# Four joint edits to a macaron kernel of four layers: the first mixture's routing in program order and its table between the experts, a pipelined weight product, another combine and lag, and an expert input built slice by slice

## The chip, the core and the metric

The kernel runs on one core of a Trainium2 chip. The metric is the device time of one launch in microseconds (us). The core has a matrix engine (TensorE, PE in the profile), a vector engine (VectorE, DVE), a scalar engine (ScalarE, ACT), a general engine (GpSimd, POOL) and a queue engine that only issues transfers (SyncE, SP). Each engine executes its own list of instructions in order; semaphores let one wait for another. Everything is fp32.

## The reference

x is 4 sequences of 512 tokens with 128 features. Four layers follow; each is a half-weighted feed-forward part, an attention (or a scan), and the same feed-forward part again with the same weights:

```python
x = x + 0.5 * _L0_ffn_ref(_layernorm(x), ...)   # Switch mixture: 8 experts, one choice, capacity 320
x = x + _L0_attn_ref(_layernorm(x), ...)        # 16 heads, a table of relative positions
x = x + 0.5 * _L0_ffn_ref(_layernorm(x), ...)
x = x + 0.5 * _L1_ffn_ref(_layernorm(x), ...)   # SwiGLU mixture: all 8 experts, two chosen, and a shared one
x = x + _L1_attn_ref(_layernorm(x), ...)        # factorised scores
x = x + 0.5 * _L1_ffn_ref(_layernorm(x), ...)
x = x + 0.5 * _L2_ffn_ref(_layernorm(x), ...)   # 8 linear experts, top two
x = x + _L2_attn_ref(_layernorm(x), ...)        # decay scan
x = x + 0.5 * _L2_ffn_ref(_layernorm(x), ...)
x = x + 0.5 * _L3_ffn_ref(_layernorm(x), ...)   # mixture, two choices a token, capacity 512
x = x + _L3_attn_ref(_layernorm(x), ...)
x = x + 0.5 * _L3_ffn_ref(_layernorm(x), ...)
```

A mixture of layer 0 or 3 does, for each token: logits of 8 experts, a softmax, the best expert (or two), the token's place within that expert by a running count over all tokens, and, if the place is under the capacity, relu(token w1 + b1) w2 + b2, weighted with the softmax value. In layer 2 an expert is linear, so its two weights can be multiplied into one 128x128 matrix beforehand. The table of layer 0's attention adds `table[t - s]` per head to the scores.

## The kernel before

**Mixtures.** The four mixture passes of layers 0 and 3 are objects named f00, f01 (layer 0) and f30, f31 (layer 3). Their names end the names of tiles, shown in the profile without numbers as `_f`. A pass has these stages.

- `empty` and `clear` (L288, L293) write zeros into two DRAM areas: disp, where tokens are put in the order of experts, and res, where answers are put in the order of tokens.
- `tokens` (L296) handles one or more sequences and yields between steps: GpSimd writes token numbers beside the tokens (L307); `norms` (L160) makes statistics on VectorE (L168, L169), the inverse root on GpSimd (L172, L173, and L176, L177 where ScalarE will apply it), and the normalised rows on VectorE, ScalarE, both, or GpSimd, as the argument `on` says; TensorE transposes (L195) and multiplies with the gate (lg, L330); VectorE picks the expert (mx, eq, first, masks; L344, L228 to L234); a scan and three small products count the places (pre L362, rank L373 to L379); VectorE makes the row to write to (kept, at, slot, to; L400 to L409); GpSimd sends the rows with one indirect transfer per 128 tokens and choice (L416), 16 for layer 0 and 32 for layer 3. Sequences depend on each other only through `cum`, the running count.
- `experts` (L426) fetches an expert's rows from disp on SP's queue (`fetch`, L443, two experts ahead), transposes them (`prepare`, L452: dT), multiplies with w1 (h, L487, 8 products of 128x320 for an expert of layer 0), bias and relu on ScalarE and VectorE, prepares the next expert, calls `beside` if there is one, multiplies with w2 (o, L523), adds the bias, weights, and sends the answers out by an indirect transfer (L509). With two choices, an expert's rows are in two halves, d and d2, filled from opposite ends; `prepare` multiplies the second with 0 or 1 (`behind`) and adds it to the first.
- `combine` (L533) reads the answers of a sequence back (r) and adds them to x.

**Order.** Most of the kernel is given to a scheduler that orders each engine's instructions by readiness within pools; `tc.manual_schedule(engines=...)` keeps the order of the program on the engines that it names. `skewed(gens, lag)` (L1519) goes round several step-by-step parts: part i joins in round i x lag. `whole` runs a part to its end. PSUM's 8 banks and the staging pool `stage` (5 buffers named raw) are handed round in order.

**The launch** (L1554 to L1570). The relative positions are fetched, disp is zeroed, then four parts `choices`, one for each sequence, are made, with norms on ScalarE and VectorE in turn. The first runs four steps; then comes the second part of `prep_table` (L945), which zeroes the table on VectorE (L953), sums the embeddings and writes the rows to DRAM (tab_rows); then all expert weights (`moe_weights`, L542, fetches in pairs of experts); then the zeros of res; then the rest of the choices, two steps apart. Behind that comes the last part of `prep_table`: eight times, two heads are fetched as overlapping rows (rev), turned over by one product (turned, L976) and copied into the table. `prep_l0_attn` transposes the attention's weights, and `padded_values` fills vpad with GpSimd (L582). Only then come f00's experts.

**After f01** (L1579 to L1603). `prep_l2` fetches layer 2's weights while f01's experts run, as their `beside`. When they are done it takes, for each expert, four transposes (wo2T, L1326), a copy that goes to ScalarE or VectorE in turn (`copy`, L131), four accumulating products (m, L1331), and a copy. A sigmoid of one column is put on ScalarE (L1585), which loads the table of that function ahead of its use. Then `combine` adds f01's answers to all four sequences, and `l1_ffn` runs for the two pairs of sequences, the second pair 12 rounds behind the first: norms (n), transposes (T), logits (lg, L1066), the up products (gu, L1151, L1152), the choice of two experts (`chosen`, L1075: comb), the transpose of that (gT, L1127), which goes through DRAM to be spread (rows, cb), and the down products (o, L1186). The first pair is `followed` by the beginning of layer 1's attention.

**f30's choices** (L1612 to L1623). Sequences 0 and 1 route inside the chain of layer 2. Sequences 2 and 3 route at its end, the second three steps behind the first, with GpSimd's order that of the program.

Of the kernel before, what the change touches and what calls it, by code (L numbers as in the profile page):

```python
# [17 lines left out]
P = 128  # L18
# [5 lines left out]
E = 8  # L24
# [17 lines left out]
def kernel(ctx: ExitStack, tc: tile.TileContext, a: dict, out: bass.AP):  # L42
# [202 lines left out]
    class Mixture:  # L245
# [180 lines left out]
        def experts(self, w, beside=None):  # L426
# [3 lines left out]
            with tc.tile_pool(name=f"moe_{self.tag}", bufs=2) as pool:  # L430
# [21 lines left out]
                def prepare(e):  # L452
                    tag = f"{e}_{self.tag}"
                    d = got[e, 0]
                    if self.k == 2:
                        d2 = got[e, 1]
                        nc.vector.tensor_tensor(d2, d2, bc(behind[:, e, :], [P, per, W]), ALU.mult)
                        nc.vector.tensor_tensor(d[:, :, :D], d[:, :, :D], d2[:, :, 2:], ALU.add)
                        nc.vector.tensor_tensor(d[:, :, D:], d[:, :, D:], d2[:, :, :2], ALU.add)
                    ps = bank(f"dT{tag}")  # L460
                    for s in range(per):
                        m = min(P, cap - s * P)
                        nc.tensor.transpose(ps[:, s * P : s * P + m], d[:m, s, :D], ident[:m, :m])
                    dT = pool.tile([P, cap], FP, name=f"dT{tag}", tag="dT")
                    nc.scalar.copy(dT, ps[:, :cap])  # L465
# [479 lines left out]
    def prep_table(pool):  # L945


        rel = stage.tile([P, D], FP, name="rel", tag="rel", bufs=1)
        nc.sync.dma_start(rel, a["L0_attn_rel_pos_emb"][P - 1 : 2 * P - 1, :])
        yield  # L950

        table = pool.tile([P, NH, S], FP, name="table", tag="table", bufs=1)
        nc.vector.memset(table[:, :, : S - 2 * P], 0.0)  # L953
# [12 lines left out]
        yield  # L966

        for h in range(0, NH, 2):

            rev = stage.tile([P, 2, 2 * P], FP, name=f"rev{h}", tag="raw")  # L970
            nc.sync.dma_start(
                rev,
                bass.AP(tensor=rows.tensor, offset=rows.offset + h * 3 * P, ap=[[1, P], [3 * P, 2], [1, 2 * P]]),
            )
            ps = bank(f"turned{h}")
            nc.tensor.matmul(ps, flip, rev.rearrange("p h s -> p (h s)"), start=True, stop=True)  # L976
            copy(table[:, h : h + 2, S - 2 * P :], ps.rearrange("p (h s) -> p h s", h=2))
        l0["table"] = table
        yield

    def prep_l0_attn():
        qkv = head_weights(a["L0_attn_qkv_w"], a["L0_attn_qkv_b"], "l0")
# [313 lines left out]
    def prep_l2(pool):  # L1296

        l2["gate"] = load_T(a["L2_ffn_w_gate"], E, D, "gate2T")
        l2["w_in"] = load(a["L2_attn_W_in"], [P, 2 * D], "win2")
        l2["w_out"] = load(a["L2_attn_W_out"], [P, D], "wout2")  # L1300
        l2["b_out"] = load_row(a["L2_attn_b_out"], "bout2")
        l2["b_in"] = load_T(a["L2_attn_b_in"].rearrange("(k d) -> k d", k=2), 2, D, "bin2T")
        yield

        m = pools["w"].tile([P, E, D], FP, name="m2", tag="m2")
        l2["m"] = m
        got = {}

        def fetch(e):
            wi, wo = raw[:, 0, e].rearrange("p (c d) -> p c d", d=D), raw[:, 1, e]  # L1310
            nc.sync.dma_start(wi, a["L2_ffn_w_in"][e].rearrange("(c f) d -> f c d", f=P))
            nc.sync.dma_start(wo, a["L2_ffn_w_out"][e])
            got[e] = wi, wo

        raw = pool.tile([P, 2, E, FF], FP, name="raw2", tag="raw2")
        for e in range(E):

            behind = yield
            nc.gpsimd.tensor_copy(raw[0:1, :, e, 0], behind[0:1, 0:1].to_broadcast([1, 2]))
            fetch(e)  # L1320
        yield
        for e in range(E):
            wi, wo = got[e]
            ps = bank(f"wo2T_{e}")
            for c in range(NC):
                nc.tensor.transpose(ps[:, c * P : (c + 1) * P], wo[:, c * P : (c + 1) * P], ident)  # L1326
            woT = pool.tile([P, FF], FP, name=f"wo2T_{e}", tag="woT", bufs=3)
            copy(woT, ps)
            pm = bank(f"m2_{e}")
            for c in range(NC):  # L1330
                nc.tensor.matmul(  # L1331
                    pm[:, :D], wi[:, c, :], woT[:, c * P : (c + 1) * P], start=(c == 0), stop=(c == NC - 1)
                )
            copy(m[:, e, :], pm[:, :D])

    def l2_ffn(pool, i, bs):
        tag = f"f2{i}_{bs[0]}"
# [215 lines left out]
    with tc.tile_pool(name="tables", bufs=1) as tables:  # L1553
        f00 = Mixture("f00", CAP0, 1)  # L1554
        f00.zeroed(stage, "raw", 5)
        made = prep_table(tables)
        next(made)
        whole(f00.empty())
        with tc.tile_pool(name="routing00", bufs=2) as pool:
# [12 lines left out]

        f30 = Mixture("f30", CAP3, 2)
        l0_attn(f00.combine, emptied(f01, f30), lambda b: f01.tokens([b], gate0T, fine=True))
    with tc.tile_pool(name="weights12", bufs=1) as mid:
# [7 lines left out]
            whole(made)  # L1583
        first = small.tile([P, 1], FP, name="first_sigmoid", tag="first_sigmoid", bufs=1)
        nc.scalar.activation(first, l2["m"][:, 0, 0:1], AF.Sigmoid)  # L1585
        for b in range(NB):
            whole(f01.combine(b))
        with tc.tile_pool(name="ahead1", bufs=2) as ahead:
            vpads[:] = [padded(ahead, 0), None]
            begun = l1_begin(ahead)  # L1590

            def followed(pool, bs):
                yield from l1_ffn(pool, 0, bs)
                if bs[0] == 0:

                    yield from begun[0](0)
                    for g in range(2):
                        begun[1](0, g)
                        yield
                        begun[4][0, g] = begun[2](0, g)  # L1600

            with tc.tile_pool(name="ffn10", bufs=2) as pool:
                whole(skewed([followed(pool, bs) for bs in pairs], 12))  # L1603

            early = []
            with tc.tile_pool(name="gates10", bufs=1) as pool:
                l1_attn(
                    lambda _: prep_l3_ffn(xs[0]), begun,
                    lambda b: l1_early(pool, pairs[0], early) if b == 1 else iter(()),
                )  # L1610

        def behind(pool, bs):  # L1612
            yield from l1_ffn(pool, 1, bs, early if bs[0] == 0 else None)
            yield from l2_ffn(pool, 0, bs)
            yield from l2_attn(pool, bs)
            yield from l2_ffn(pool, 1, bs)
            if bs[0] == 0:

# [77 lines left out]
```

## Time and profile before

| | us |
|---|---|
| time before, median of 3 (1512.09 to 1516.94) | 1515.85 |
| the profiled execution | 1516.03 |
| its span, and what lies outside it | 1514.3, 1.7 |
| PE busy, of the span | 1278.2 (84%) |
| VectorE, ScalarE, GpSimd busy | 881.6, 682.6, 696.5 |
| mean granted TensorE clock | 0.914 |
| routing of f00; its experts | 0 to 62; 62 to 112 |
| layer 0's attention | 115 to 346 |
| f01's scatters and experts; prep_l2's products | 346 to 423; 419 to 443 |
| first feed-forward part of layer 1; its attention | 423 to 520; 520 to 820 |
| chain of layers 1 to 2; f30's scatters and experts | 820 to 972; 972 to 1084 |
| layer 3's attention; f31 | 1084 to 1395; 1395 to 1515 |

The page lists the busy time of each engine, the span in 40 slices, the chain of work that ended last (each step followed back to what released it), and the costliest groups. In a row of the timeline, the columns are start, duration, engine, line, operation, result, operands with their shapes, and count; in brackets stands how long the engine sat idle before it and what ended that. These rows of the page belong to the stages above:

```profile
L509 POOL DMA_INDIRECT res_f<-y_f,back_f x112 | 109.7, 980 | 127.6 <-ACT y_f L508 91.3
L416 POOL DMA_INDIRECT disp_f<-n_f,to_f x96 | 95.1, 991 | 55.8 <-issue 37.1
L487 PE MATMUL h_f<-dT_f,w_l 128*128 128x320 f32 (+1 forms) x256 | 104.0, 544 | 2.8 <-ACT dT_f L465 2.8
```

They read: 96 scatters kept GpSimd busy for 95.1 us, 991 ns each; and TensorE waited only 2.8 us in all ahead of the 256 first products of the experts, all of it for the copy of dT.

### The profile page before, as it was taken

How to read it: one execution, taken by the hardware profiler on the slowest of the kernel's cores; microseconds unless marked ns; L12 is line 12 of the kernel's file. 1: busy time of each engine (PE TensorE's matmuls, PEld its weight loads, DVE VectorE, ACT ScalarE, POOL GpSimd, SP SyncE). 2: the span in 40 equal slices, each digit the busy share in tenths (PEclk: the TensorE clock that was granted, in tenths of full speed). 3: DMA queues.
4: the chain of work that ended last, by engine and by line, in shares of the span. 5: the costliest groups of instructions: out<-in, count | busy, mean ns of one | idle time of the engine just before them, and what ended most of it. 6: DMA issues, size and time to landing. Idle time of an engine off the chain costs nothing.

```text
span 1514.3 us, 28772 instructions
## 1 busy us (share of the span) xinstructions
PE 1278.2 (84%) x10645; PEld 817.5 (54%) x10645; DVE 881.6 (58%) x2893; ACT 682.6 (45%) x1431; POOL 696.5 (46%) x808
## 2 busy tenths in 40 slices
PE   4687999995968989998999878739589999998394
PEld 3464666774755656676656656627333434343273
DVE  5336777663356657777566755434287787772343
ACT  1235877871422367776621222104336555563041
POOL 5346767871533578876443112555520323202253
PEclk9898999996989999999999887759799999998597
DMA  8410240002412874241130000032114000000223
GB/s 259 104 53 22 79 171 11 9 7 78 147 36 57 230 241 151 85 142 36 38 76 1 1 0 3 29 90 85 49 42 149 9 12 5 15 1 15 78 82 108
DMA packets 100660, 106.21 MB, mean 70 GB/s; under 512 B 9084, under 2 KB 73832, under 8 KB 100520
## 3 DMA queue, kind: packets, MB, share of 16 engines
q1 hardware_dynamic: 91752, 90.11, 20.7%
q0 software_dynamic: 6656, 13.22, 2.5%
q8 instruction: 84, 1.38, 0.4%
q10 hardware_dynamic: 2112, 1.05, 0.3%
q14 instruction: 56, 0.46, 0.1%
HBM read 62.49 MB, written 41.85 MB: 69 GB/s over the span
## 4 chain that ended last, share of the span: by engine, by line
PE 66%; DVE 9%; POOL 8%; issue 7%; DMA 6%; ACT 2%; SPq 1%; POOLq 0%; ACTq 0%; DVEq 0%
PE s_a L618 13%; PE t_a L663 8%; PE h_f L487 5%; PE acc_a L757 5%; PE o_f L523 5%; PE acc_a L685 5%; PE y_f L1380 4%; PE t_a L618 3%; PE ot_a L776 2%; POOL disp_f L416 2%; POOL res_f L509 2%; PE gate_f L1397 2%; PE lg_f L330 1%; PE T_f L195 1%; DVE low L707 1%
## 5 line engine op out<-in xcount | busy, mean ns | idle before, releaser
L650 POOL TENSOR_SCALAR sc_a<-sc_a,top_a 128x128 f32<-128x128 f32 (+3 forms) x256 | 276.5, 1096 | 84.4 <-DVE top_a L635 58.5
L618 PE MATMUL s_a<-k_a,q_a 32*128 32x512 f32 (+3 forms) x1536 | 262.7, 540 | 5.4 <-DVE top_a L639 3.5
L727 ACT ACTIVATE w_a<-t_a 128x512 f32<-128x512 f32 x256 | 140.2, 595 | 124.2 <-PE t_a L618 92.1
L707 DVE TENSOR_REDUCE low<-s_a 128x1 f32<-128x512 f32 x256 | 163.4, 684 | 47.8 <-PE t_a L618 34.8
L663 PE MATMUL t_a<-ident,sc_a 128*128 128x128 f32 x1280 | 170.9, 279 | 6.1 <-DVE top_a L639 5.3
L618 PE MATMUL t_a<-ql_a,k_a 32*128 32x512 f32 x512 | 169.7, 648 | 0.5 <-DVE low L707 0.2
L509 POOL DMA_INDIRECT res_f<-y_f,back_f x112 | 109.7, 980 | 127.6 <-ACT y_f L508 91.3
L663 PEld LDWEIGHTS t_a<-ident,sc_a 128*128 128x128 f32 x1280 | 142.1, 142 | 41.2 <-issue 15.6
L652 ACT ACTIVATE sc_a<-sc_a,top_a 128x128 f32<-128x128 f32 (+3 forms) x256 | 134.8, 575 | 13.9 <-DVE top_a L639 13.4
L618 PEld LDWEIGHTS s_a<-k_a,q_a 32*128 32x128 f32 x1536 | 92.0, 185 | 77.7 <-issue 42.5
L672 ACT ACTIVATE w_a<-t_a 128x256 f32<-128x256 f32 (+2 forms) x192 | 94.3, 526 | 68.7 <-PE t_a L663 68.2
L416 POOL DMA_INDIRECT disp_f<-n_f,to_f x96 | 95.1, 991 | 55.8 <-issue 37.1
L523 PE MATMUL o_f<-w_l,h_f 128*128 128x128 f32 (+1 forms) x896 | 110.5, 278 | 1.4 <-ACT h_f L491 1.0
L523 PEld LDWEIGHTS o_f<-w_l,h_f 128*128 128x128 f32 (+1 forms) x896 | 102.3, 184 | 10.3 <-DVE back_f L472 4.4
L487 PE MATMUL h_f<-dT_f,w_l 128*128 128x320 f32 (+1 forms) x256 | 104.0, 544 | 2.8 <-ACT dT_f L465 2.8
L685 PE MATMUL acc_a<-w_a,vpad 128*32 128x128 f32 x2560 | 97.6, 278 | 0.6 <-ACT w_a L672 0.6
L674 ACT COPY w_a<-t_a 128x256 f32<-128x256 f32 (+2 forms) x192 | 93.3, 526 | 5.7 <-PE t_a L663 5.3
L172 POOL TENSOR_SCALAR rs_f<-mv_f 128x4 f32<-128x4 f32 (+1 forms) x23 | 5.3, 232 | 194.8 <-DVE mv_f L169 194.3
L639 DVE CUSTOM_DVE_ANT_0 sc_a<-s_a,future 128x128 f32<-128x128 f32 (+3 forms) x128 | 62.3, 487 | 45.0 <-PE s_a L618 41.4
L639 DVE CUSTOM_DVE_ANT_0 sc_a<-s_a,table 128x128 f32<-128x128 f32 (+3 forms) x128 | 62.5, 488 | 44.0 <-PE s_a L618 33.6
L757 PE MATMUL acc_a<-w_a,vpad 128*32 128x256 f32 x1024 | 84.8, 400 | 2.8 <-ACT w_a L727 1.9
L508 ACT ACTIVATE y_f<-o_f,d_f 128x128 f32<-128x128 f32 (+1 forms) x112 | 39.0, 394 | 103.5 <-DVE o_f L503 92.4
(344 smaller groups left out, 2227.3 us busy)
## 6 DMA issues: line engine op xcount, KB each, us to landing
fac_a<-fac_a_sb SPq DMA_DIRECT2D x36, 256.0 KB
disp_f<-zeros_f SPq DMA_DIRECT2D x4, 2080.0 KB
d_f<-disp_f SPq DMA_DIRECT2D x32, 260.0 KB
w_l<-in_L_ffn_w_dram SPq DMA_DIRECT2D x16, 512.0 KB
cb_f<-rows_f SPq DMA_DIRECT2D x16, 512.0 KB
q_a<-fac_a SPq DMA_DIRECT2D x32, 256.0 KB
k_a<-fac_a SPq DMA_DIRECT2D x32, 256.0 KB
r_f<-res_f SPq DMA_DIRECT2D x16, 256.0 KB
```

What stands on the lines that cost most here:

```text
L416: nc.gpsimd.indirect_dma_start(out=self.to[c][i0 + t][:, :], out_offset=bass.IndirectOffsetOnAxis(ap=to[:, c, t : t + 1], axis=0), in_=ns[ ...
L487: nc.tensor.matmul(ps[u][:, :cap], w1[:, e, (c + u) * P : (c + u + 1) * P], dT, start=True, stop=True)
L509: nc.gpsimd.indirect_dma_start(out=self.back[e * per + s][:, :], out_offset=bass.IndirectOffsetOnAxis(ap=back[:m, s : s + 1], axis=0), in_ ...
L523: nc.tensor.matmul(po[:m, s, :], h[:, c, s * P : s * P + m], w2[:, e, c, :], start=(c == 0), stop=(c == NC - 1),)
L618: nc.tensor.matmul(ps[:, n0:n1], q[r : r + SLOT, i * P : (i + 1) * P], k[r : r + SLOT, n0:n1], start=True, stop=True)
L650: nc.gpsimd.tensor_scalar(sc, sc, top, None, ALU.subtract)
L652: nc.scalar.activation(sc, sc, AF.Exp, bias=top, scale=-1.0)
L663: nc.tensor.transpose(ps[:, x * n + j * P : x * n + (j + 1) * P], st["sc", u, i, r0 + x][:, j * P : (j + 1) * P], ident,)
L685: nc.tensor.matmul(st["acc", u][r * SLOT : (r + 1) * SLOT, i * P : (i + 1) * P], vpads[b % 2][:, j, g * 4 + r, :], st["w", u, i, r][:, j * ...
L707: nc.vector.tensor_reduce(st["low", u][:, i, c : c + 1], ps, AX.X, ALU.max, negate=True)
L727: nc.scalar.activation(w, ps, AF.Exp)
L757: nc.tensor.matmul(acc[r * SLOT : (r + 1) * SLOT, n0:n1], vpads[b % 2][:, j, g * 4 + r, :], st["w", u, j, r][:, n0:n1], start=(j == 0 and ...
```

## The change

1. **The launch.** The weights' first four steps, the zeros of res and all four choices now stand first, with every norm on ScalarE. TensorE, VectorE, ScalarE and GpSimd keep the program's order there. The rest of the weights (the transposes of b1), the table's zeros, its rows and GpSimd's fills of vpad stand behind the choices. The table's last part is cut into four, of two turned products each, and put between f00's experts by `beside`: nothing at the first expert, two products after each of the next four, and the attention's weights after the sixth. SP is not among the engines held in order.
2. **prep_l2.** The transposes of expert e stand ahead of the products of expert e - 1. All its copies are ScalarE's.
3. **combine and lag.** f01's answers for sequences 2 and 3 are added inside the second pair's part, which takes two rounds for it; the lag of the pairs is 10 instead of 12, so the second pair's `l1_ffn` begins in the same round as before.
4. **f30.** Sequence 3 runs four steps behind sequence 2 instead of three.
5. **prepare with two choices.** d + behind x d2 is made by one fused operation for each of the four slices of 128 tokens, and the product and sum of the two leading columns are made behind them.

```diff
-                        nc.vector.tensor_tensor(d2, d2, bc(behind[:, e, :], [P, per, W]), ALU.mult)
-                        nc.vector.tensor_tensor(d[:, :, :D], d[:, :, :D], d2[:, :, 2:], ALU.add)
+                        for s in range(per):
+                            nc.vector.scalar_tensor_tensor(
+                                d[:, s, :D], d2[:, s, 2:], behind[:, e, s : s + 1], d[:, s, :D], ALU.mult, ALU.add
+                            )
+                        nc.vector.tensor_tensor(d2[:, :, :2], d2[:, :, :2], bc(behind[:, e, :], [P, per, 2]), ALU.mult)
                         nc.vector.tensor_tensor(d[:, :, D:], d[:, :, D:], d2[:, :, :2], ALU.add)
...
             copy(table[:, h : h + 2, S - 2 * P :], ps.rearrange("p (h s) -> p h s", h=2))
+            if h % 4:
+                yield
         l0["table"] = table
-        yield
...
-        for e in range(E):
-            wi, wo = got[e]
-            ps = bank(f"wo2T_{e}")
...
-            copy(woT, ps)
...
-            copy(m[:, e, :], pm[:, :D])
+        wT = {}
+        for e in range(E + 1):
+            if e < E:
+                ps = bank(f"wo2T_{e}")
+                for c in range(NC):
+                    nc.tensor.transpose(ps[:, c * P : (c + 1) * P], got[e][1][:, c * P : (c + 1) * P], ident)
+                wT[e] = pool.tile([P, FF], FP, name=f"wo2T_{e}", tag="woT", bufs=3)
+                nc.scalar.copy(wT[e], ps)
+            if e > 0:
+                pm = bank(f"m2_{e - 1}")
...
+                nc.scalar.copy(m[:, e - 1, :], pm[:, :D])
...
-            choices = [f00.tokens([b], gate0T, "vector" if b % 2 else "scalar", pool) for b in range(NB)]
-            for part in choices[:1] * 4:
-                next(part)
-            next(made)
-            whole(first_weights())
+            tc.manual_schedule(engines={E_.PE, E_.DVE, E_.Activation, E_.Pool}),
+        ):
+            choices = [f00.tokens([b], gate0T, "scalar", pool) for b in range(NB)]
+            weights = first_weights()
+            for _ in range(E // 2):
+                next(weights)
             f00.clear()
             whole(skewed(choices, 2))
-        whole(made)
-        prep_l0_attn()
-        padded_values(tables)
-        f00.experts(l0["w"])
+            whole(weights)
+            next(made)
+            padded_values(tables)
+
+        def behind_experts():
+
+            yield
+            yield from made
+            prep_l0_attn()
+            yield
+
+        beside = behind_experts()
+        f00.experts(l0["w"], lambda _: next(beside, None))
...
-        for b in range(NB):
+        for b in pairs[0]:
             whole(f01.combine(b))
...
             def followed(pool, bs):
+                if bs[0] > 0:
+                    for b in bs:
+                        yield from f01.combine(b)
                 yield from l1_ffn(pool, 0, bs)
...
-                whole(skewed([followed(pool, bs) for bs in pairs], 12))
+                whole(skewed([followed(pool, bs) for bs in pairs], 10))
...
-                yield from skewed([f30.tokens([b], l3["gate"], "scalar", pool) for b in bs], 3)
+                yield from skewed([f30.tokens([b], l3["gate"], "scalar", pool) for b in bs], 4)
```

More of the change, by code (lines that the diff above doesn't have):

```diff
@@ L1321, in prep_l2 @@
         yield
-        for e in range(E):
-            wi, wo = got[e]
-            ps = bank(f"wo2T_{e}")
-            for c in range(NC):
-                nc.tensor.transpose(ps[:, c * P : (c + 1) * P], wo[:, c * P : (c + 1) * P], ident)
-            woT = pool.tile([P, FF], FP, name=f"wo2T_{e}", tag="woT", bufs=3)
-            copy(woT, ps)
[L1329 to L1333, printed above, removed]
-            copy(m[:, e, :], pm[:, :D])
+        wT = {}
[8 more added lines that the diff above has]
+                pm = bank(f"m2_{e - 1}")
+                for c in range(NC):
+                    nc.tensor.matmul(
+                        pm[:, :D], got[e - 1][0][:, c, :], wT[e - 1][:, c * P : (c + 1) * P],
+                        start=(c == 0), stop=(c == NC - 1),
+                    )
+                nc.scalar.copy(m[:, e - 1, :], pm[:, :D])
     def l2_ffn(pool, i, bs):
@@ L1558 @@
         whole(f00.empty())
-        with tc.tile_pool(name="routing00", bufs=2) as pool:
-            choices = [f00.tokens([b], gate0T, "vector" if b % 2 else "scalar", pool) for b in range(NB)]
-            for part in choices[:1] * 4:
-                next(part)
-            next(made)
-            whole(first_weights())
+        E_ = mybir.EngineType
+        with (
+            tc.tile_pool(name="routing00", bufs=2) as pool,
+            tc.manual_schedule(engines={E_.PE, E_.DVE, E_.Activation, E_.Pool}),
[4 more added lines that the diff above has]
+                next(weights)
             f00.clear()
             whole(skewed(choices, 2))
-        whole(made)
-        prep_l0_attn()
-        padded_values(tables)
-        f00.experts(l0["w"])
+            whole(weights)
[8 more added lines that the diff above has]
+        f00.experts(l0["w"], lambda _: next(beside, None))
         f01 = Mixture("f01", CAP0, 1)
```

## The prediction

> **What bounds the kernel now.** I read the page's fourth part first, then busy time by stretch, then the timeline at the four places that the diff touches.
>
> ```profile
> PE 66%; DVE 9%; POOL 8%; issue 7%; DMA 6%; ACT 2%; SPq 1%; POOLq 0%; ACTq 0%; DVEq 0%
> ```
>
> The reader sees that two thirds of the chain that ends last is TensorE, and a third is hand-overs. An edit can gain only where TensorE starves. Columns of the next view: stretch, its length, busy time (and instructions) of PE, PEld, DVE, ACT, POOL, granted clock, DMA share, GB/s.
>
> ```profile
> 0.00:62.00 62.00, 29.58 (x98) 19.76 (x98) 27.81 (x151) 9.66 (x21) 29.22 (x54) 0.92 0.75 209
> 370.00:423.00 53.00, 50.68 (x299) 38.79 (x300) 18.13 (x51) 21.62 (x51) 24.05 (x32) 0.96 0.45 134
> 423.00:473.00 50.00, 36.61 (x167) 24.05 (x166) 27.18 (x82) 12.54 (x29) 11.79 (x16) 0.86 0.28 64
> 972.00:1010.00 38.00, 8.77 (x40) 7.30 (x39) 11.32 (x67) 2.96 (x8) 23.97 (x35) 0.55 0.22 64
> ```
>
> The launch, the stretch after f01's experts and f30's scatters leave TensorE idle for 32, 13 and 29 us: there is room. The second row, an expert stage, has 2.3 us to spare: whatever is put there is paid.
>
> **Part A: the launch.** Timeline of the launch and of its end:
>
> ```profile
> 1.96 3.47 DVE L953 MEMSET table<- 128x4096 f32 x1 [0.79 <-issue]
> 7.20 1.80 POOL L582 MEMSET vpad<- 128x2048 f32 x1
> 10.01 0.38 POOL L307 TENSOR_SCALAR n_f<-tok_id 128x4 f32<-128x4 f32 x1 [1.01 <-DVE tok_id L105]
> 29.77 1.24 POOL L416 DMA_INDIRECT disp_f<-n_f,to_f  x1 [5.55 <-DVE masks_f L234]
> ...
> 57.16 3.70 PE L976 MATMUL turned<-rev,flip 128*128 128x512 f32 x4 [8.68 <-DMA rev<-tab_rows]
> ...
> 62.65 2.42 PE L487 MATMUL h_f<-dT_f,w_l 128*128 128x320 f32 x8 [0.64 <-ACT dT_f L465]
> ```
>
> x has landed by 4.25, but VectorE begins its statistics at 5.37, behind the table's memset; GpSimd fills vpad at 7.20 and again near 12.4 ahead of the norms. At the end the tokens of expert 0 are there at 54.65, and TensorE takes them at 61.43, since two turned pairs (57.16, waiting for their fetch) and the attention's weights stand in front.
>
> Afterwards, by in-order queues: statistics of sequences 0 and 1 from 4.3 to 7.3; tok_id 8.0; GpSimd's n_f 0.38, rs 0.22, rstd 1.05, off 0.23 to 10.2; ScalarE's norm 1.65 to 11.9; last transpose and copy 1.1 to 13.05; logits 1.88 to 15.0; eight choice steps of about 0.2 to 16.3. Then sequence 3's norm stands, in program order, ahead of the first place numbers: VectorE's to at 22.3, GpSimd's rstd and copy to 23.5. First scatter about 24.0, **5.8 earlier**. Sixteen scatters took 20.9 (29.77 to 50.66), so 44.9; the fetch went out 1.93 later and took 2.06: landed 48.85.
>
> From there f01 is the model, the same stage without a table: its tokens landed at 370.05, and the first read-back of its answers at 425.84 (VectorE's L539), 55.8 later. On top come eight turned pairs, at 0.86 each (two 128x512 products start every 0.86 at full clock, L1151 at 462.13 and L1152 at 463.00): 6.9; and 0.7 for the attention's weights. TensorE has no slack there, so both are paid: 48.85 + 55.8 + 7.6 = 112.3, against 115.4 before (the chain's r_f at 112.53, 2.86 long). The cold first product is in this model: f01's took 3.88 where the old f00's, warmed by the table, took 2.42. **A gains 3.1**, the 5.8 and the 6.7 of waiting less 7.6, less the 1.9 of cold clock (products and transposes). Ends: a first scatter no earlier than before loses 2.7; a scatter at 20 and a table that half fits beside ScalarE's waits gains 8. I take 3, since each term has a row.
>
> Costed at nothing: VectorE's memset and GpSimd's vpad fills, put behind the choices. The scatters (GpSimd 0.96 in every 1.26) and the wait for landing hide them; uncovered they cost 3.5 each. [...] I take 0.
>
> SP's order: all weights go ahead of the res zeros; the first three expert fetches go ahead of the table's rows and its eight fetches, and experts 3 and 4 stand behind the sixth to eighth of these, which wait for staging buffers that turned releases.
>
> **Part B: prep_l2 and combine.**
>
> ```profile
> 420.19 1.16 PE L1331 MATMUL m<-wo2T,raw 128*128 128x128 f32 x8 [0.78 <-DVE wo2T L134]
> 421.19 0.60 PE L1326 MATMUL wo2T<-ident,raw 128*128 128x128 f32 x4
> 422.57 1.16 PE L1331 MATMUL m<-wo2T,raw 128*128 128x128 f32 x8 [0.78 <-DVE wo2T L134]
> ...
> 442.48 1.44 PE L195 MATMUL T_f<-ident,n_f 128*128 128x128 f32 x8
> ```
>
> Each expert costs transposes, a wait of 0.78 for the copy, products: 2.38, growing to 4.4 where VectorE and ScalarE are in the norms (441.51 waited 2.90). With transposes one ahead, the wait goes: 8 x 1.76 = 14.1 from 418.75 gives 432.8; ScalarE, which now does all copies (0.59 + 0.27 an expert, under 1.76), also loads a table (1.28 at 421.67) and runs the norms between them: 1.2 each. T starts at 435.2 instead of 442.5: 7.3. Combine of sequences 2 and 3 is moved behind the pair 0, 1, so VectorE's add and statistics fall into the pair's choices, and n_f_2 waits for GpSimd's rstd ahead of the last comb product: new, about 2 us (rstd took 1.68 at 432.94; VectorE's own n_f waited 1.52). Queued behind it are comb and gT, for which TensorE waits (457.36, idle 3.50). So **B gains 5.5**, 2 to 8: below, if the clock, 0.86 here, is no better and the wait grows to 5; above, if the wait lies in TensorE's gu products. TensorE is in order from there into the attention of layer 1, so the gain stays.
>
> **Part C: skew 4.** In f30, to of sequence 2 was ready at 981.00, behind mx of sequence 3, which waited for its logits till 980.35:
>
> ```profile
> 980.35 0.19 DVE L344 TENSOR_REDUCE mx_f<-lg_f 128x4 f32<-128x32 f32 x1 [1.20 <-PE lg_f L330]
> 982.03 1.12 POOL L416 DMA_INDIRECT disp_f<-n_f,to_f  x1 [6.12 <-DVE masks_f L234]
> ```
>
> Now TensorE's rank_2 goes ahead of T_3 (1.63) and lg_3 (1.82): to at 978.3, scatter at 979.3. The 16 scatters behind are GpSimd's alone (1.26 each), so the stage moves whole: **2.6**, from 0 to 3.2.
>
> **Part D: prepare of k=2.**
>
> ```profile
> 1008.29 0.70 DVE L457 TENSOR_TENSOR d_f<-d_f,behind_f 128x520 f32<-128x520 f32 x1 [3.07 <-DMA d_f<-disp_f]
> 1009.03 0.69 DVE L458 TENSOR_TENSOR d_f<-d_f,d_f 128x512 f32<-128x512 f32 x1
> 1010.03 1.09 PE L463 MATMUL dT_f<-ident,d_f 128*128 128x128 f32 x4 [23.26 <-DMA d_f<-disp_f]
> ```
>
> TensorE starts 1.74 after VectorE and ends at 2.83. A 128x128 operation takes 0.29 (L503), so four end at 1.16, each freeing one transpose: the last ends near 1.75. 1.1 gained at the first expert of f30 and of f31: **2.2**, 0.5 to 2.8. [...] I take 2.2.
>
> **Sum:** 3.1 + 5.5 + 2.6 + 2.2 = 13.4. The profiled execution took 1516.03 (span 1514.3 and 1.7 around it), 0.2 above the median of 1515.85: **1503**. About 0.3%, 4.5 us, is what a measurement of this kernel can tell: faster is below 1511.3, slower above 1520.4.
>
> **Cases.**
> - Forecast, 1498 to 1509: 0.50.
> - More, 1496: sequence 3's norm isn't late and comb's wait is covered (A 8, B 8). For it: each is a wait, not work. Against it: program order. 0.10.
> - **B is given back and A is nil**: cb's transfer (10.25 in the chain at 462.47) and n_f_2's wait take the place of T's, and the first scatter waits for zeros behind 8 MB of traffic (DMA share 0.75 before 62). A 0, B 2, C 2.6, D 2.2: 1509, up to 1513. 0.25, of it 0.10 within 0.3%.
> - **Slower: the table's last fetches.** The sixth to eighth are issued only as turned frees buffers, about one expert (6.3: 50.68 busy over eight) ahead of need, and experts 3 and 4 queue behind them on SP; all later experts stand behind turned on TensorE. It decides from a landing that takes longer than those 6.3. At three times the 4.40 that such a fetch took (the chain at 52.63), each stalls 6.9, 21 in all: 1524; half of that is 1513. For it: the 8.68 wait at 57.16 is this fetch. Against it: 4.40 was seen at a DMA share of 0.75, and the fifty us that follow have 0.19. 0.13, of it 0.02 within.
> - The order written down is not what sets the work (other waits hold it): 1516, 0.02.
>
> Faster 0.75, same 0.14, slower 0.11. The range 1495 to 1515 leaves out the slower case and the edges of the others, 0.19.
>
> **What will show it.** A: first scatter near 24, h at full length 3.9 near 50.5, the first read-back near 112; a turned product that waits for rev speaks for the slower case. B: m products following transposes without the 0.78, T near 435 on the old time axis less A. C: 16 scatters with no gap before sequence 2's. D: first transposes 0.5 after VectorE's first operation. Wrong if TensorE's busy share in f00's experts falls, or if gT waits over 6.

## The result, and the profile after

Over nine runs of each kernel on one chip, the median went from 1513.49 us (1511.48 to 1517.83) to 1508.56 us (1501.87 to 1511.05): a ratio of 0.9953, 95% interval 0.9938 to 0.9967, which is 5.0 to 9.4 us, 7.1 in the middle (the two medians themselves lie 4.9 apart). The profiled execution took 1508.99 us (span 1507.3), 7.0 less than the profiled one of before. The changed kernel is faster, by about half of the 13.4 us that were forecast; its median lies inside the range of 1495 to 1515.

First the chain that ended last, as the page of the changed kernel gives it.

```profile
PE 67%; DVE 9%; issue 7%; POOL 7%; DMA 5%; SPq 2%; ACT 2%; POOLq 0%; ACTq 0%; DVEq 0%
```

TensorE's share is up by one point, GpSimd's and the transfers' are each down by one. Next the busy time in the same four stretches as before (stretch, its length, busy time and instructions of PE, PEld, DVE, ACT and POOL, granted clock, DMA share, GB/s).

```profile
0.00:62.00 62.00, 30.27 (x124) 23.17 (x125) 27.16 (x143) 15.06 (x35) 32.46 (x60) 1.00 0.69 190
370.00:423.00 53.00, 52.17 (x309) 40.12 (x309) 15.93 (x44) 21.75 (x51) 23.91 (x32) 0.95 0.42 126
423.00:473.00 50.00, 40.13 (x183) 27.68 (x184) 24.46 (x86) 16.52 (x37) 15.43 (x20) 0.83 0.28 64
972.00:1010.00 38.00, 12.08 (x40) 8.76 (x41) 13.76 (x77) 4.00 (x9) 22.74 (x32) 0.51 0.30 85
```

TensorE's idle time in the third row falls from 13.4 to 9.9 us. The launch holds 124 TensorE instructions where it held 98, although the turned products have left it but for the start of the first: the experts begin sooner. The timeline (start, duration, engine, line, operation, and in brackets the idle time before and what ended it) shows each part. The launch:

```profile
24.40 1.24 POOL L416 DMA_INDIRECT disp_f<-n_f,to_f  x1 [0.58 <-POOL n_f L413]
...
37.62 3.47 DVE L956 MEMSET table<- 128x4096 f32 x1 [0.80 <-issue]
...
39.56 0.96 POOL L416 DMA_INDIRECT disp_f<-n_f,to_f  x1 [0.30 <-issue]
...
49.97 0.95 PE L466 MATMUL dT_f<-ident,d_f 128*128 128x128 f32 x3 [8.00 <-DMA d_f<-disp_f]
51.56 3.95 PE L490 MATMUL h_f<-dT_f,w_l 128*128 128x320 f32 x8 [0.64 <-ACT dT_f L468]
...
61.63 1.99 PE L979 MATMUL turned<-rev,flip 128*128 128x512 f32 x4
...
113.34 0.69 DVE L542 TENSOR_TENSOR x<-x,r_f 128x512 f32<-128x512 f32 x1 [6.71 <-DMA r_f<-res_f]
```

The same read-back before:

```profile
115.41 0.69 DVE L539 TENSOR_TENSOR x<-x,r_f 128x512 f32<-128x512 f32 x1 [6.78 <-DMA r_f<-res_f]
```

The first scatter starts at 24.40 instead of 29.77, the tokens are taken at 49.97 instead of 61.43, turned stands between the experts and waits for no fetch, and the first read-back is added at 113.34 instead of 115.41. The table's memset runs beside the scatters, and the one at 39.56 keeps its 0.96 and its gap of 0.30.

Layer 2's product and the first feed-forward part of layer 1, first two rows of before:

```profile
418.75 0.66 PE L1326 MATMUL wo2T<-ident,raw 128*128 128x128 f32 x4
...
457.36 1.86 PE L1127 MATMUL gT_f<-ident,comb_f 128*8 128x128 f32 x8 [3.50 <-issue]
```

and after:

```profile
418.15 1.09 PE L1332 MATMUL wo2T<-ident,raw 128*128 128x128 f32 x8
...
421.08 1.06 PE L1338 MATMUL m<-wo2T,raw 128*128 128x128 f32 x8
421.97 0.60 PE L1332 MATMUL wo2T<-ident,raw 128*128 128x128 f32 x4
424.22 1.16 PE L1338 MATMUL m<-wo2T,raw 128*128 128x128 f32 x8 [1.65 <-ACT wo2T L1334]
...
434.15 1.92 PE L195 MATMUL T_f<-ident,n_f 128*128 128x128 f32 x8
...
451.11 0.34 DVE L186 TENSOR_SCALAR n_f<-x,mv_f,rstd_f 128x128 f32<-128x128 f32 x1 [1.90 <-POOL rstd_f L173]
451.37 0.22 DVE L1093 TENSOR_TENSOR comb_f<-comb_f,total_f 128x64 f32<-128x64 f32 x1
...
451.69 1.86 PE L1131 MATMUL gT_f<-ident,comb_f 128*8 128x128 f32 x8 [6.47 <-issue]
```

The wait of 0.78 per expert is gone, but for 0.40 ahead of the first product and for two places where ScalarE, which makes all copies now, is late: 1.65 here, behind its load of a table (1.28), and 2.18 further on, among its norms. T starts 16.0 us behind the first wo2T instead of 23.7. In exchange sequence 2's norm waits 1.90 for GpSimd's inverse root, the last comb product stands behind it, and TensorE idles 6.47 ahead of gT instead of 3.50.

f30, its first scatter of the last sixteen and its first expert:

```profile
977.28 1.12 POOL L416 DMA_INDIRECT disp_f<-n_f,to_f  x1 [3.25 <-ACT nT_f L321]
...
1004.21 1.14 DVE L458 SCALAR_TENSOR_TENSOR d_f<-d_f,behind_f,d_f 128x128 f32<-128x128 f32 x4 [3.66 <-DMA d_f<-disp_f]
1004.87 1.08 PE L466 MATMUL dT_f<-ident,d_f 128*128 128x128 f32 x4 [19.84 <-DMA d_f<-disp_f]
1006.75 5.50 PE L490 MATMUL h_f<-dT_f,w_l 128*128 128x512 f32 x8 [0.80 <-ACT dT_f L468]
```

GpSimd's wait ahead of these scatters is 3.25 instead of 6.12, and h starts 2.54 behind VectorE's first operation on d, where it took 3.63.

### The profile page after: what moved, and what is told of

Read it like the earlier page. It is cut to its first block, busy times and chain, and to the rows that moved or that the text cites. A ratio compares the mean times of both kernels' runs of the same rounds, so it can differ in the third digit from the quotient of the medians.

```text
span 1507.3 us, 28840 instructions
## 1 busy us (share of the span) xinstructions
PE 1281.6 (85%) x10645; PEld 821.5 (54%) x10645; DVE 873.4 (58%) x2924; ACT 689.9 (46%) x1448; POOL 692.6 (46%) x812
## 4 chain that ended last, share of the span: by engine, by line
PE 67%; DVE 9%; issue 7%; POOL 7%; DMA 5%; SPq 2%; ACT 2%; POOLq 0%; ACTq 0%; DVEq 0%
PE s_a L621 13%; PE t_a L666 8%; PE h_f L490 5%; PE acc_a L688 5%; PE acc_a L760 5%; PE o_f L526 5%; PE y_f L1388 4%; PE t_a L621 3%; PE ot_a L779 2%; PE gate_f L1405 2%; POOL res_f L512 2%; PE o_f L1190 1%; PE gu_f L1155 1%; DVE low L710 1%; POOL disp_f L416 1%
```

## The experiments

Every kernel is compared with the kernel before, run on the same chip. Three chips were used here, which differ by more than the change does (1518.06, 1495.88 and 1496.45 us for the kernel before), so only ratios are compared between them.

**Each part alone.** Four kernels make one part of the diff shown above each, and leave the rest as before.

*The launch* (point 1 of the change):

```diff
-            choices = [f00.tokens([b], gate0T, "vector" if b % 2 else "scalar", pool) for b in range(NB)]
+            choices = [f00.tokens([b], gate0T, "scalar", pool) for b in range(NB)]
...
+            whole(weights)
+            next(made)
```

> The launch alone (choices in program order, table between the experts), the rest as before. Theory 1, the places add up: first scatter near 24.4, first read-back of f00's answers near 113.3 against 115.4, and the whole time about 2 us (0.13%) below before. Rival, the products of the table are paid and nothing is gained because the stage behind it only waits longer: 0 us. Rival, the edit gives TensorE a colder start that costs again later: above before.

*The product and combine* (points 2 and 3):

```diff
-        for e in range(E):
+        for e in range(E + 1):
...
-                whole(skewed([followed(pool, bs) for bs in pairs], 12))
+                whole(skewed([followed(pool, bs) for bs in pairs], 10))
```

> The pipelined weight product of layer 2 with the moved combine and lag 10, the rest as before. Theory 1 (what the trace of after shows at layer 1's attention stays): about 5 us (0.33%) below before, gT of the first pair about 5.5 earlier after f01's last product. Rival (the lead is given back in layer 1's attention and the chain, where after took 2.4 and 1.1 us longer than before): about 2 us below. If that give-back is only the clock that this one execution was granted, the attention of layer 1 lasts 229 to 232 us here whatever the lead.

*The skew* (point 4):

```diff
-                yield from skewed([f30.tokens([b], l3["gate"], "scalar", pool) for b in bs], 3)
+                yield from skewed([f30.tokens([b], l3["gate"], "scalar", pool) for b in bs], 4)
```

> Sequence 3 of f30 four steps behind sequence 2, the rest as before. Theory: the first of the last 16 scatters starts 2.7 us earlier after the chain's last product, everything behind moves with it, 2.7 us (0.18%) below before. Rival: hidden behind GpSimd, 0.

*The slices* (point 5):

```diff
-                        nc.vector.tensor_tensor(d2, d2, bc(behind[:, e, :], [P, per, W]), ALU.mult)
+                        for s in range(per):
+                            nc.vector.scalar_tensor_tensor(
```

> The fused slices in prepare alone, the rest as before. Theory: 1.1 us at the first expert of f30 and 1.0 at that of f31 (VectorE's first operation to the first product: 3.63 to 2.54 and 3.37 to 2.42), together 2 us (0.14%) below before; no change in the other 14 experts. [...]

| part alone | ratio to before (95%) | what its trace shows at its place, us |
|---|---|---|
| launch | 0.9989 (0.9969 to 1.0009) | first scatter 24.41 for 29.77; first read-back 114.65 for 115.41 |
| product, combine | 0.9951 (0.9930 to 0.9973) | wo2T to T 16.6 for 23.7; gT waits 6.48 for 3.50 |
| skew | 0.9974 (0.9949 to 0.9998) | end of the chain to first scatter 8.47 for 11.32; scatter to VectorE's first d 26.95 for 26.26 |
| slices | 0.9992 (0.9971 to 1.0014) | d to h 2.57 for 3.63 (f30), 2.43 for 3.37 (f31) |

At its place each part does in its own kernel what it does in the changed one, so nothing there hinges on their combination. (The launch's read-back came at 114.65, not near 113.3 as expected.) Only the product with its combine, and just the skew, can be told from no change by time; for the launch and the slices the gain is shown at their places alone. The four ratios add up to 0.94% less, with an interval of some 0.44% to either side (the root of the summed squares); the whole change measured 0.47% on its own chip.

**The product alone, and combine alone.** These split the largest part. The product is point 2 without point 3:

```diff
+                wT[e] = pool.tile([P, FF], FP, name=f"wo2T_{e}", tag="woT", bufs=3)
+                nc.scalar.copy(wT[e], ps)
+            if e > 0:
+                pm = bank(f"m2_{e - 1}")
```

> Only the pipelined product of layer 2's weights, with f01's answers still added to all four sequences ahead of the first pair and the lag of 12 (part 2 of the change without part 3). Theory (the product's waits are the gain, and part 3 gives about 2 us of it back through the new wait in front of comb): from the first wo2T to the first T_f some 16.0 as in the kernel with both parts (before: 23.73), the gap ahead of gT back at 3.5 instead of 6.47, and from wo2T to layer 1's first s_a 93 to 94 or less, against 101.1 before and 92.9 with both; ratio about 0.995. Rival (part 3 is worth something itself, since the two extra sums sit ahead of the first norms on VectorE): first T_f at 17.5 or later behind wo2T, s_a at 95 or later, ratio about 0.997.

Combine is point 3 without point 2:

```diff
-        for b in range(NB):
+        for b in pairs[0]:
...
+                if bs[0] > 0:
+                    for b in bs:
+                        yield from f01.combine(b)
```

> Only part 3 of the change: f01's answers for sequences 2 and 3 are added inside the second pair's part, lag 10; the product of layer 2's weights stays as it was. Theory: nothing is won at the first T_f (about 23.7 behind wo2T as before), and the norm of sequence 2 stands in front of comb with its wait of 1.9, so that s_a comes 1 to 2 us later than before (102 to 103 behind wo2T); ratio 1.000 to 1.002. Rival (the sums that leave the front of the first pair bring its norms forward): first T_f at 22.5 or earlier, s_a no later than 100.5, ratio 0.998 to 1.000.

Measured: product 0.9971 (0.9957 to 0.9985), combine 0.9991 (0.9974 to 1.0008). The timeline of the kernel with the product alone:

```profile
428.00 2.05 PE L1334 MATMUL m<-wo2T,raw 128*128 128x128 f32 x16
432.84 1.45 PE L195 MATMUL T_f<-ident,n_f 128*128 128x128 f32 x4 [2.79 <-DVE n_f L186]
435.01 1.09 PE L195 MATMUL T_f<-ident,n_f 128*128 128x128 f32 x4 [0.72 <-DVE n_f L186]
...
449.39 1.86 PE L1127 MATMUL gT_f<-ident,comb_f 128*8 128x128 f32 x8 [3.15 <-issue]
```

With VectorE adding four sequences ahead of the first norms, TensorE is through with the products early and then waits 2.79 for n: the norms, not the products, end last there. T still comes 15.1 behind wo2T, and the gap ahead of gT is short again, as the theory had it. Layer 1's first s_a stands 94.1 behind wo2T (101.1 before), which is the theory's value too; the ratio is the rival's. For combine alone the rival held at each point: T 21.9 behind wo2T, s_a 95.6 behind it, and a time that can't be told from no change. So the product is what the large part gains by. Moving combine takes load from VectorE ahead of the norms and adds the wait ahead of gT; which of the two is larger the times do not settle, and the traces have to be compared at like clock (next section).

**How far unchanged code varies.** From wo2T to s_a the unchanged code took 101.1, 97.6, 96.7 and 102.8 us in the profiles of before, the launch, the skew and the slices. Most of that is seen in the granted clock. Busy time by stretch, from the first T to the last product ahead of gT, in the kernel before:

```profile
442.00:453.80 11.80, 11.80 (x38) 7.45 (x37) 3.97 (x8) 3.63 (x8) 3.10 (x4) 0.57 0.00 1
```

and in the kernel with combine alone, whose products there are the same:

```profile
441.30:448.10 6.80, 6.56 (x35) 4.10 (x33) 2.90 (x13) 3.04 (x8) 5.34 (x8) 1.00 0.01 2
```

and in the changed kernel:

```profile
434.15:445.00 10.85, 10.85 (x33) 7.19 (x32) 2.47 (x6) 2.85 (x6) 2.96 (x4) 0.55 0.09 26
```

At a clock of 0.57 these products took 11.8 us, at 1.00 they took 6.6. So one profile is 4 to 5 us uncertain here, and only profiles with a like clock in this stretch (here from each one's first T) can be compared:

| kernel | clock of the stretch | wo2T to s_a, us |
|---|---|---|
| before; slices | 0.55; 0.53 | 101.1; 102.8 |
| changed | 0.56 | 96.5 |
| product alone | 0.51 | 94.1 |
| launch; skew | 0.92; 1.00 | 97.6; 96.7 |
| points 2 and 3 alone; changed, run again; table under the scatters (both below) | 0.87; 0.91; 0.90 | 92.9 each |
| combine alone | 1.00 | 95.6 |

Points 2 and 3 together gain 5.5 us at the lower clock and 4.3 at the higher. Combine moved on its own gains some 1.5. On top of the product it seems to give back 2.4 (94.1, then 96.5), about the 2 us of the theory; these are single profiles. (The three at 92.9 come from two chips.)

These rows show a clock near one half, and a difference between executions at one place. What makes the clock fall and rise they do not show: in the kernel before, the products kept TensorE busy without a break from 443 to 453, at a clock of 0.50, before it rose (0.87 from 453.0 to 453.8).

**After it, once more, and two waits taken away.** On another chip the changed kernel was run again unedited.

> The changed kernel once more, for its spread and as the measure of the next three. If the 3.1 us that its first trace lost between the start of layer 1's attention and the chain's last sum belong to the edit, that stretch is again 453.5 to 454.5 long here; if they are the clock of one execution, it falls anywhere between 450.8 and 455.3, where the kernels with unchanged code fell. Time 0.4 to 0.7% below before.

It measured 0.9936 (0.9916 to 0.9955), 9.6 us, within the range. Its first scatter stands at 24.30, and s_a 92.9 behind wo2T. The stretch from s_a to the chain's last sum took 445.2 us, outside both of the ranges that were expected: on this chip and on the third, all eight profiles have 442.4 to 445.4, whichever code they run; on the result's chip and the first they have 450.8 to 455.3. What makes this difference between chips was not looked for. The third chip answers the question asked: with the old code 443.6 and 445.2 (product alone, combine alone), with the changed code 444.9 and 442.4 (the norm on GpSimd and the table early, below). So the edit costs nothing there.

Next the table's part goes under the scatters: its rows are written after three rounds of choices, its fetches go out on ScalarE's queue, and nothing of it is left between the experts.

```diff
-            whole(skewed(choices, 2))
-            whole(weights)
+            rounds = skewed(choices, 2)
+            for _ in range(3):
+                next(rounds)
             next(made)
+            whole(rounds)
+            whole(weights)
+            whole(made)
...
-            nc.sync.dma_start(
+            nc.scalar.dma_start(
```

> After, with the table's rows made while VectorE waits for the first logits, its eight fetches on ScalarE's queue and its eight products and copies under the scatters, ahead of the experts; the attention's weights stay between experts. Theory (the eight products between the experts are paid in full, 7.7 us, and TensorE idles from 36 to 50): first read-back of f00's answers near 105.5 instead of 113.3, 7 to 8 us (0.5%) less than after. Rival (the fetches of the table land too late or delay the scatters): TensorE waits for rev at 50 and most of it is lost, 0 to 3 us less than after.

It measured 0.9925 (0.9908 to 0.9943), not to be told from the changed kernel beside it; the first read-back came at 113.75, for 114.69. The rival held. Its timeline on TensorE, and below it on ScalarE and its queue:

```profile
48.33 1.10 PE L984 MATMUL turned<-rev,flip 128*128 128x512 f32 x2 [1.09 <-DMA rev<-tab_rows]
55.74 3.49 PE L984 MATMUL turned<-rev,flip 128*128 128x512 f32 x4 [6.31 <-DMA rev<-tab_rows]
59.06 0.59 PE L466 MATMUL dT_f<-ident,d_f 128*128 128x128 f32 x3
60.28 2.15 PE L490 MATMUL h_f<-dT_f,w_l 128*128 128x320 f32 x7 [0.64 <-ACT dT_f L468]
...
51.54 0.37 ACTq L975 DMA_DIRECT2D rev<-tab_rows  x1
51.95 0.59 ACT L985 COPY table<-turned 128x512 f32<-128x512 f32 x1 [5.81 <-DMA d_f<-disp_f]
```

Six of the eight turned products ran under the scatters. The last two fetches went out only at 51.5, behind a wait on ScalarE, whose queue issues them; the profile names the landing of d as what ended it. They landed at 55.7, and all experts stood behind them. This is the forecast's slower case in small: a table fetch that comes late holds everything behind it on TensorE. ScalarE's copy ahead of the issue had ended at 46.1, so 5.4 us passed before the issue and some 4 in transfer, where all eight fetches took 4.1 to 5.1.

Then the wait ahead of comb: the norm of sequences 2 and 3 goes to GpSimd, so that VectorE has nothing queued in front of comb.

```diff
-        yield from norms([xs[b] for b in bs], ns, tag, "both")
+        yield from norms([xs[b] for b in bs], ns, tag, "gpsimd" if tag == "f10_2" else "both")
```

> After, with the norm of sequences 2 and 3 in layer 1's first feed-forward part applied by GpSimd, so that neither VectorE's last comb product nor ScalarE's copy of gT stands behind it. Theory (the 1.90 us wait ahead of comb is on the path): gT about 33.5 - 2.1 = 31.4 us after f01's last product, the gap before it 4.4 instead of 6.5, 2 us (0.14%) less than after. Rival (the wait is covered, or GpSimd's norm delays its own products): same as after.

It measured 0.9887 (0.9871 to 0.9904). Again, on a third chip:

> The changed kernel with the norm of sequences 2 and 3 in the first feed-forward part of layer 1 applied by GpSimd, once more and on another chip than the first time. If the edit is worth the 2 to 3 us that the trace shows at gT and s_a, the ratio lies at 0.991 to 0.994, between the changed kernel's 0.995 or 0.994 less 0.0015 to 0.002; if the first time's 0.9887 is what the edit brings, at 0.987 to 0.990.

0.9893 (0.9859 to 0.9926): in the second of the two ranges, with an interval that reaches into the first. The timeline there:

```profile
445.09 1.57 PE L1131 MATMUL gT_f<-ident,comb_f 128*8 128x128 f32 x8 [4.35 <-issue]
```

gT waits 4.35 instead of 6.47 and comes 28.2 behind wo2T, for 30.7 in the changed kernel run again: some 2.1 to 2.4 us are won at the place, and 3.1 at s_a (89.7 behind wo2T for 92.9). In this edit's first profile, whose stretch ran at 0.54, less is seen beside the changed kernel's at 0.56: gT 32.9 for 33.5 and s_a 95.2 for 96.5. The ratio of 0.9887, beside the 0.9936 of the same chip, says 7 us, more than the place shows. The runs with this edit also had a higher mean clock than the kernel before beside them (0.922 for 0.916 on the one chip, 0.921 for 0.916 on the other), where the changed kernel had 0.920; whether the edit brings that itself was not tried, and the cause of the rest stays open. Both edits together:

> Both of these on top of after. If the two places are separate: 9 to 10 us (0.6%) less than after, near 0.989 of before. If the lead of one is lost in later waits: less than the sum.

0.9914 (0.9892 to 0.9936), no better than the norm alone; the last two fetches were late there as well (TensorE waited 6.79 for them).

**The table early, with buffers of its own.** Last, the late fetch is taken away: rows and fetches go out on ScalarE's queue between routing steps, in two transfers of eight heads, each into its own buffer. The norm by GpSimd is kept.

```diff
+            next(rounds)
+            next(made)
+            for _ in range(3):
+                next(rounds)
+            next(made)
+            whole(rounds)
+            whole(made)
+            whole(weights)
...
-            rev = stage.tile([P, 2, 2 * P], FP, name=f"rev{h}", tag="raw")
+            rev = l0["rev_pool"].tile([P, HALF, 2 * P], FP, name=f"rev{g}", tag=f"rev{g}", bufs=1)
```

> The same norm by GpSimd, and the whole table built under f00's scatters: its rows are written and fetched from ScalarE's queue, the fetch in two transfers of eight heads into buffers of their own, issued between the routing steps of sequences 2 and 3, so that no product waits for a buffer. f00's experts have no table products between them. Theory: the eight turned products run between about 36 and 50 while TensorE waits for the scatters, dT starts near 50 with no wait for rev, the first h runs in 2.4 to 3.9, and the first read-back of f00 stands at 105 to 108, against 113.3 after; 6 to 8 us less than the kernel with GpSimd's norm alone, ratio 0.984 to 0.988. Rival: the fetch of 2 MB shares its engines with the scatters and the experts' weights and lands after 45, so that dT waits for it to 55 or so, or the scatters stretch; then at most 3 us are won, ratio 0.988 to 0.992.

It measured 0.9852 (0.9829 to 0.9876), a median of 1476.62 us beside 1496.45 before and 1481.18 for the norm alone, and it is the lowest ratio of all; its interval lies below both of the changed kernel's, but overlaps those of the norm alone, so by time the step beyond the norm is not settled. TensorE in its launch, in the timeline:

```profile
35.90 9.46 PE L987 MATMUL turned<-rev,flip 128*128 128x512 f32 x16
...
50.38 0.95 PE L466 MATMUL dT_f<-ident,d_f 128*128 128x128 f32 x3 [4.84 <-DMA d_f<-disp_f]
51.97 4.63 PE L490 MATMUL h_f<-dT_f,w_l 128*128 128x320 f32 x8 [0.64 <-ACT dT_f L468]
...
108.14 0.69 DVE L542 TENSOR_TENSOR x<-x,r_f 128x512 f32<-128x512 f32 x1 [6.79 <-DMA r_f<-res_f]
```

All eight turned pairs lie in the time in which TensorE waits for the scatters, dT waits for tokens alone, and the read-back is 6.0 ahead of the same kernel without this edit (114.15), just outside the 105 to 108 that was expected; h took 4.63, not the 2.4 to 3.9. The scatters kept 0.96 in 1.26 although the transfers' share was 0.87 up to 50. Queue, order, size of the fetches and buffers were changed at once; which of them was needed was not tried.

## Why the prediction was right, and where its sizes were off

At each of the four places the mechanism was the one that was forecast; the sum was too large.

**A, 3.1 forecast.** From the tokens to the first read-back the forecast put 55.8 + 7.6 = 63.4, and the profile has just that, 49.97 to 113.34. To the tenth this is luck: the changed kernel run again and the two profiles with the norm on GpSimd, all with this launch, took 64.1 to 64.9, and in them h took 4.63, here 3.95 (3.88 in the model). The long first h of the model was there, but the recorded clock does not explain it in this profile: it was 1.00 over the 3.95, where it was 0.61 over f01's 3.88 and 1.00 over f00's 2.42 in the kernel before. A turned pair cost 0.96 instead of 0.86, 0.8 over eight, which was made good elsewhere here. The other term that was mis-sized is the landing, forecast at 48.85: the first scatter was 0.4 late, the sixteen took 21.4 instead of 20.9, and the tokens came 4.2 behind the last instead of 4.0. In the profiled pair 2.1 is left. Over six profiles with the old launch (115.1 to 116.2, mean 115.5) and five with the new (113.34, 114.65, 114.69, 114.96, 114.15, mean 114.4) it is 1.2. The memset hid behind the scatters, as costed (the scatter at 39.56 kept its 0.96 and 0.30).

**B, 5.5 forecast, 4.6 in the profiled pair, 4.3 to 5.5 at like clock.** T came 7.7 earlier for 7.3, and the new wait stands where it was put, 1.90 for "about 2". By the prediction's own mark, "wrong if gT waits over 6", it would have failed, since gT waited 6.47. The wait had grown by 3.0: with the norm on GpSimd it is 4.35, so 2.1 of it is the new wait; the rest goes with TensorE coming to the place earlier. The mark was badly chosen, as a gap can grow where the work ahead of it is done sooner. The forecast took the stretch at its clock of before and named the clock only as a reason for less, without saying that the same products may take 5 us more or less (11.8 us at 0.57 and 6.6 at 1.00, above).

**C, 2.6 forecast.** 2.7 came at the first scatter, and 0.7 of it was gone at VectorE's first operation on d: net 2.0 (2.2 in the skew's own kernel). That "the stage moves whole" was the part that didn't hold. The sixteen scatters kept their length (19.7 from first to last start, before and after); from the last of them to d it is 7.2 instead of 6.6, in the skew's own kernel too. What takes the 0.6 was not tried.

**D, 2.2 forecast.** 1.09 and 0.95 were measured at the first h, 2.0. The four fused operations took 1.14 for 1.16. Behind that h a part may be given back: on the second and third chips, from the first h to the experts' last product, f30 took 62.0 and f31 61.9 in the mean of six profiles with the slices, for 61.7 each in the two without. That would leave some 1.4.

Together that is 9.5 to 11.8 us at the places, for 13.4. In the profiled pair it is 10.7, and the whole execution shows 7.0: 0.3 was lost in layer 0's attention, 1.2 in f01's experts, where the first h took 4.63 instead of 3.88, and 3.1 between layer 1's first s_a and the end of the chain, all in unchanged code; 0.9 more was won behind f30's first h. The first h of f01 before:

```profile
371.71 3.88 PE L487 MATMUL h_f<-dT_f,w_l 128*128 128x320 f32 x8 [0.59 <-ACT dT_f L465]
```

and after:

```profile
369.91 4.63 PE L490 MATMUL h_f<-dT_f,w_l 128*128 128x320 f32 x8 [0.59 <-ACT dT_f L468]
```

The kernel with the product alone, whose edit lies behind this place, has 4.54 there; the changed kernel run again has 4.63, and the last kernel 4.08. Busy time by stretch of layer 1's attention before:

```profile
519.90:749.50 229.60, 213.35 (x2632) 150.81 (x2633) 155.54 (x657) 163.62 (x356) 169.81 (x167) 0.98 0.37 116
```

and after:

```profile
514.70:746.70 232.00, 215.48 (x2632) 152.44 (x2633) 155.11 (x658) 163.13 (x356) 169.47 (x167) 0.97 0.37 114
```

The same 2632 products took 2.1 us more at a clock of 0.97 for 0.98. From s_a to the end of the chain the kernel with the skew alone, whose code there is that of before, took longer still than the changed one (455.3 for 454.0; before 450.8), and on the third chip old and changed code took the same (above), so this is the spread of executions, not a price of the edit. On the second chip the 9.6 us (6.7 to 12.6) hold the sum at the places; on the result's own chip the interval ends at 9.4, just below it.

**The rivals.** The slower one, late table fetches, fell: no turned product waited for rev, with the transfers' share at 0.28 between 62 and 112. It came true in small in the kernel with the table under the scatters, through a fetch that was issued late. That B is given back and A is nil was half right for A and wrong for B; that its 1509 lies next to the measured 1508.6 is luck.

## What to carry to other kernels

Fill the time in which an engine waits for a fixed transfer with work that would stand in its way later, and give that work its transfers ahead of time, so that they wait neither for a queue nor for a buffer: the same table cost 0.96 per pair between the experts, and under the scatters it put the tokens 0.4 later in all (50.38 for 50.01). In a loop of product, copy, product, put the next one's first product ahead of the wait (0.78 per expert here). Price a gain at one place with the granted clock of that place in several profiles: here the same products took 6.6 us or 11.8.

## What was not expected of the hardware

After 4.3 to 8.0 us without a product, the eight products of 128x320 that open a mixture took from 3.9 to 4.6 us in different executions, and 2.42 where they followed products closely. Where turned ran at full clock (1.00) up to 45.3 and TensorE then idled for 4.84, the first products ran at half clock (0.50) again (busy time by stretch of the last kernel, the wait and then the first expert):

```profile
45.50:50.40 4.90, 0.06 (x2) 0.06 (x1) 0.19 (x1) 0.48 (x1) 4.55 (x5) 0.70 0.41 113
50.40:57.20 6.80, 6.16 (x14) 3.58 (x14) 2.07 (x8) 1.48 (x3) 0.00 (x0) 0.50 0.25 65
```

The times of one kernel follow its mean granted clock: fitted over all runs on each chip, with a constant for each kernel, 0.001 less of the clock goes with 0.9 to 1.0 us more, and what then remains scatters by 1.2 to 1.6 us (the changed kernel's nine runs: 1501.87 at 0.920, 1511.05 at 0.913). This is a correlation; no run set the clock.
